# A two-layer expert MLP on one core: the last product of three layer-0 pairs is made due at 16.5 instead of 18 units

## The chip, the cores and the metric

The kernel runs on one core of one Trainium2 chip. The metric is the time of one execution on the device in microseconds (us), lower is better; the time given for a kernel is the median of several executions. The engines are named as in the profile: PE (TensorE, matmuls), PEld (its weight loads), DVE (VectorE), ACT (ScalarE), POOL (GpSimd), SP (SyncE, which issues most DMAs). PSUM is the accumulator memory that PE writes, in banks; SBUF is the working memory of all the engines.

## The reference, cut to what matters

```python
# x: (16, 256, 256); cond: (16, 8); hidden sizes 512 (layer 0) and 1024 (layer 1)
# layer 0: one expert for each batch, chosen by argmax
expert = argmax(cond, -1)
up   = einsum('bsd,bhd->bsh', x, W_up[expert])   + b_up[expert]
gate = einsum('bsd,bhd->bsh', x, W_gate[expert]) + b_gate[expert]
x = x + einsum('bsh,bdh->bsd', silu(up) * gate, W_down[expert]) + b_down[expert]
# layer 1: the two best experts of eight for each batch, weighted, and a shared MLP
mlp = lambda x, g, u, d: (gelu(x @ g) * (x @ u)) @ d
x = x + sum_k w[b, k] * mlp(x, skill[sel[b, k]]) + mlp(x, shared)
```

All of it is float32.

## The kernel before, in words

**Pairs.** Batches that use the same expert are put together two at a time (`Pair`); leftovers run alone (`Single`). The order of the batches is sorted on the chip. For a pair each weight product is a 2x2 block product, and the kernel makes it with seven products and some sums instead of eight products (Strassen's way, in Winograd's form; the table `STEPS`, lines 40 to 48, gives for each of the seven steps its PSUM bank tag, its weight block and its data block). Two kinds of such products follow each other:

- the first product (gate and up together), in quarters `j` of the hidden size: 2 quarters in layer 0, 4 in layer 1. `Pair.up(j, k)` (line 533) is step k of quarter j. In this text it is **Uk**. It takes two matmuls by the program, four by the profile's count, and afterwards issues copies on ACT (`copy`, line 522) or combinations on DVE (`combine`, line 526: `c<-cp,Y` or `c<-cp,Q`).
- the last product, `Pair.down(k)` (line 587), here **Dk**, k = 0 to 6. Its matmuls are on line 597. D0, D2 and D4 all add into the one bank with tag A, D1 and D5 open a bank with tag Y (two in turn, shared with U1 and U5), D3 and D6 use the one bank B. After D0, D2 and D4 the helper `early` reads the bank A into a `dz` tile, in layer 0 on DVE (line 614, which adds the bias and x). After D1, D4, D5 and D6 the helper `late` adds the other bank and writes `ys` (line 630 in layer 0, DVE). So D2 cannot start before the `early` of D0 has read bank A, and a U1 or U5 that gets D1's bank cannot start before the `late` of D1 has read it.

Sums of data blocks are made by `sums_b` (lines 472 to 474, three DVE operations): for x, called by `sums_x` (line 463), and for the activations, called by `act_sums` (line 583). `act` (line 573) makes silu(up) * gate: ACT adds the biases and takes silu (line 571), in layer 1 it takes gelu (line 577), and DVE multiplies (line 580). Sums of weight blocks run on POOL (`sums_a`, lines 479 to 482; `sums_q` for the first product, `sums_d` for the last).

**The order of the work** is written out when the program is built. Each engine then works through its own queue in that order, and waits on semaphores where it needs another engine's result. `Line` (line 832) holds a clock in units: `main` runs a step, adds its time (`UP` = 2 units for one Uk) and then calls `flush`, which runs all that was put down with `later` and has come due, the earliest due first; among equals, what was put down first. The clock is a whole even number at every flush.

For a pair that starts at clock 0 (the one before it is called its predecessor), `Pair.run` (line 661) does this:

- U0 to U5 of quarter 0 end at clocks 2, 4, ... 12, of quarter 1 at 14 ... 24.
- U6 of a quarter is due 4 units after its end, `act0(1)` 3, `act` 6, `act_sums` 12.
- The sums of the next pair's x (`sums_x`) are put down at the start of quarter 1, clock 12, due 5 later, at 17 (line 878).
- D0 to D6 of the predecessor are due at `first + step * k`, with `first` 18 (line 460) and `step` 3 in layer 0 (lines 678 to 680): at 18, 21, 24, 27, 30, 33, 36. They thus run in the second half of the next pair and the first half of the one after.
- D6 also gives the tiles back (`give`, line 639), and what waits for a tile (`when_free`, line 132), for instance the load of the next weights `d` (line 418) or an `act`, is then issued.

In this row of work layer 0 has four pairs, here **P0 to P3** (`l0_pairs`, line 783), and then comes **S0**, the first pair of the shared MLP of layer 1 (`shared[0]`). In the profile P1 starts with the U0 at 41.71 us, P2 with that at 59.79, P3 with that at 78.82 and S0 with that at 97.36.

SP's queue holds, in program order, the loads of weights (`q<-wq_dram`, `d<-wd_dram`), of x, and the stores of layer 0's results (lines 453 and 454). The load of a weight tile `d` waits until the last product that read this tile is done.

Of the kernel before, what the change touches and what calls it, by code (L numbers as in the profile page):

```python
# [59 lines left out]
def kernel(  # L60
# [722 lines left out]
    l0_pairs = [Pair(next(names), 0, 2 * i) for i in range(NP1)]  # L783
# [4 lines left out]
    pairs = [Pair(next(names), 1, 2 * i) for i in range(NP2)]  # L788
    more_pairs = [Pair(next(names), 1, 2 * NP2 + 2 * i) for i in range(MOST[1])]
    ones = [Single(next(names), 1, 2 * NP2 + i) for i in range(NS2)]  # L790
    shared[-1].last = True
    shared[-2].step = 7

# [307 lines left out]
```

## Time and profile before

| what | value |
|---|---|
| median of 3 runs | 1051.12 us (1050.55 to 1052.24) |
| the profiled execution, its time | 1051.36 us |
| the profiled execution, its span | 1049.7 us |
| PE busy | 1038.2 us, 99% of the span |
| PEld busy | 900.3 us, 86% |
| DVE busy | 777.0 us, 74% |
| ACT busy | 371.3 us, 35% |
| POOL busy | 446.7 us, 43% |
| granted PE clock | 0.999 |

The span runs from the first to the last instruction; the time of the same execution is 1.66 us longer. A busy time is the sum of an engine's instructions. Matmuls are pipelined and their ends are modelled, so it is better to look at their starts: from one step of four matmuls to the next there are 0.864 us where nothing is waited for (89.59, 90.45, 91.31 for U1, U6, U2 of P3), and any larger distance is a wait. A line of the timeline gives the start, the duration, the engine, the line of the program, the operation with output <- inputs, the shape, the count of merged instructions and, in brackets, the idle time ahead of it with what ended it.

### The profile page before, as it was taken

Reading aid. Unit: us, or ns where it says so; the run is one execution under the profiler, and the core shown is the slowest. Engines: PE = TensorE matmul, PEld = TensorE weight load, DVE = VectorE, ACT = ScalarE, POOL = GpSimd, SP = SyncE. Lnnn points to the kernel's source line nnn. Section 1 sums busy time; section 2 is a strip of 40 time slices with the busy share of each in tenths; the row PEclk is TensorE's granted clock in tenths of the full one; section 3 lists DMA queues with packets and bytes.
Section 4 is the critical chain, followed back from the end, with each engine's and each line's share of the span. In section 5 each row is a group of like instructions: output and inputs, shape, how many; then the busy total and the mean of one; then the engine's idle time right before and its main releaser. Section 6 shows DMA issues by size and latency. Waiting matters only on the chain.

```text
span 1049.7 us, 14152 instructions
## 1 busy us (share of the span) xinstructions
PE 1038.2 (99%) x4750; PEld 900.3 (86%) x4750; DVE 777.0 (74%) x1207; ACT 371.3 (35%) x583; POOL 446.7 (43%) x492
## 2 busy tenths in 40 slices
PE   9999999999999999999999999999999999999998
PEld 6778888888888888888888888888888888888886
DVE  7789978878687877887777778777766236776764
ACT  2444353535333333333333333333333123333331
POOL 2946331221043765666476556645201245630000
PEclk9999999999999999999999999999999999999999
DMA  7636656656664355345335533543655445356522
GB/s 237 241 127 203 240 181 194 207 166 236 200 235 119 88 140 140 93 109 140 98 87 138 140 98 103 140 122 83 178 159 171 133 136 156 91 180 184 183 75 45
DMA packets 60974, 157.47 MB, mean 150 GB/s; under 512 B 7506, under 2 KB 27090, under 8 KB 56658
## 3 DMA queue, kind: packets, MB, share of 16 engines
q1 hardware_dynamic: 47618, 140.90, 40.3%
q0 software_dynamic: 12976, 15.21, 9.4%
q8 instruction: 42, 0.69, 0.3%
q14 instruction: 50, 0.41, 0.1%
q10 hardware_dynamic: 288, 0.26, 0.1%
HBM read 132.23 MB, written 24.12 MB: 149 GB/s over the span
## 4 chain that ended last, share of the span: by engine, by line
PE 89%; DVE 7%; issue 2%; ACT 1%; DMA 1%; SPq 0%; DVEq 0%; ACTq 0%
PE X L541 24%; PE Q L541 16%; PE Y L541 16%; PE A L597 12%; PE B L597 9%; PE Y L597 8%; DVE c L526 2%; PE X L692 2%; PE Q L692 1%; DVE bt L580 1%; PE A L722 1%; DVE bt L472 1%; DVE bt L473 1%; PE B L722 1%; ACT c L577 1%
## 5 line engine op out<-in xcount | busy, mean ns | idle before, releaser
L522 ACT ACTIVATE cp<-X 128x512 f32<-128x512 f32 x318 | 189.5, 596 | 519.2 <-PE X L541 518.6
L580 DVE TENSOR_TENSOR bt<-c 128x1024 f32<-128x1024 f32 x106 | 145.7, 1374 | 102.8 <-ACT c L577 93.0
L541 PE MATMUL Y<-xt,q 128*128 128x256 f32 x736 | 189.8, 380 | 1.1 <-DVE c L526 0.6
L541 PE MATMUL Q<-xt,s 128*128 128x256 f32 x736 | 189.5, 380 | 0.6 <-DVE c L526 0.6
L541 PE MATMUL X<-xt,s 128*128 128x256 f32 x736 | 189.5, 380 | 0.0
L526 DVE TENSOR_TENSOR c<-cp,Q 128x512 f32<-128x512 f32 x212 | 144.3, 681 | 37.4 <-ACT cp L522 32.9
L526 DVE TENSOR_TENSOR c<-cp,Y 128x512 f32<-128x512 f32 x212 | 144.1, 680 | 22.4 <-PE Y L541 22.0
L541 PEld LDWEIGHTS Y<-xt,q 128*128 128x128 f32 x736 | 138.9, 190 | 23.2 <-DVE c L526 3.9
L451 POOL DMA_DIRECT2D out_dram<-ys x46 | 49.0, 1065 | 255.7 <-DVE ys L626 103.2
L541 PEld LDWEIGHTS Q<-xt,s 128*128 128x128 f32 x736 | 139.3, 190 | 21.2 <-DVE c L526 2.5
L541 PEld LDWEIGHTS X<-xt,s 128*128 128x128 f32 x736 | 139.3, 190 | 20.5 <-ACT cp L522 1.4
L479 POOL TENSOR_TENSOR s<-q 128x256 f32<-128x256 f32 x78 | 72.1, 924 | 131.8 <-PE Q L541 66.2
L482 POOL TENSOR_TENSOR s<-s,q 128x256 f32<-128x256 f32 x78 | 62.5, 801 | 101.0 <-PE Q L541 101.0
L597 PE MATMUL A<-bt,ds 128*128 128x256 f32 x424 | 101.5, 379 | 1.4 <-DVE dz L614 1.4
L597 PE MATMUL B<-bt,ds 128*128 128x256 f32 x424 | 101.4, 379 | 0.0
L577 ACT ACTIVATE c<-c 128x1024 f32<-128x1024 f32 x92 | 96.7, 1052 | 12.9 <-DVE c L526 12.7
L472 DVE TENSOR_TENSOR bt<-bt 128x512 f32<-128x512 f32 x113 | 95.0, 840 | 0.7 <-DMA bt<-x_dram 0.6
L541 PE MATMUL X<-xt,q 128*128 128x256 f32 x368 | 94.4, 379 | 0.0
L597 PEld LDWEIGHTS A<-bt,ds 128*128 128x128 f32 x424 | 80.4, 190 | 13.0 <-POOL s L481 1.4
L597 PEld LDWEIGHTS B<-bt,ds 128*128 128x128 f32 x424 | 80.5, 190 | 11.2 <-ACT ys L737 0.3
L597 PE MATMUL Y<-bt,d 128*128 128x256 f32 x376 | 90.0, 379 | 0.0
L597 PEld LDWEIGHTS Y<-bt,d 128*128 128x128 f32 x376 | 71.4, 190 | 9.7
(163 smaller groups left out, 1157.1 us busy)
## 6 DMA issues: line engine op xcount, KB each, us to landing
q<-wq_dram SPq DMA_DIRECT2D x114, 512.0 KB, 3.7
d<-wd_dram SPq DMA_DIRECT2D x22, 1024.0 KB, 6.6
s<-qsums SPq DMA_DIRECT2D x28, 512.0 KB, 4.9
xt<-x1d SPq DMA_DIRECT2D x46, 256.0 KB, 4.3
out_dram<-ys POOLq DMA_DIRECT2D x46, 256.0 KB, 5.1
ds<-dsums SPq DMA_DIRECT2D x7, 1024.0 KB, 6.3
d<-wd_dram SPq DMA_DIRECT2D x7, 513.0 KB, 5.1
bt<-x_dram SPq DMA_DIRECT2D x14, 256.0 KB, 4.7
```

The costliest lines, as they stand in the source:

```text
L451: nc.gpsimd.dma_start(row(out), ys[:, :, t, :], accum_op=ALU.add)
L472: tt(t[:, 4:6, :], t[:, 0:3:2, :], t[:, 2:4, :], ALU.subtract)
L479: tt(s("S1"), a("A21"), a("A22"), ALU.add)
L482: tt(s("nS4"), s("S2"), a("A12"), ALU.subtract)
L522: nc.scalar.activation(t, self.banks["X", j], AF.Copy)
L526: nc.vector.tensor_tensor(self.c[j][:, block].rearrange("p m s -> p (m s)"), self.copies[n, j], self.banks[tag, j], op,)
L541: nc.tensor.matmul(self.banks[tag, j][:, bass.ts(m, S)], lhsT=self.q[j][:, m, A_AT[a], :] if a in A_AT else self.s[j][:, m, S_AT[a], :], r ...
L577: nc.scalar.activation(u, u, AF.Gelu_apprx_tanh)
L580: nc.vector.tensor_tensor(t[:, 0:4, :], u, v, ALU.mult)
L597: nc.tensor.matmul(d, lhsT=src[:, j, :], rhs=self.acts[j][:, B_AT[b], :], start=OPENS[k] and j == 0, stop=j == self.kp - 1, skip_group_che ...
L692: nc.tensor.matmul(dst[:, bass.ts(half, S)], lhsT=self.q[j][:, m, 2 * half + c, :], rhs=self.xt[:, c, :], start=(c == 0), stop=(c == KD - 1),)
L722: nc.tensor.matmul(self.po[:, bass.ts(c, S)], lhsT=self.d[:, 2 * c + half, j, :], rhs=self.acts[j][:, bass.ts(half, S)], start=(j == 0 and ...
```

## The change

It sets the attribute `first` of the first three layer-0 pairs, P0, P1 and P2, from 18 to 16.5. P3 and all pairs of layer 1 keep 18.

```diff
     ones = [Single(next(names), 1, 2 * NP2 + i) for i in range(NS2)]
+    for u in l0_pairs[:-1]:
+        u.first = 16.5
     shared[-1].last = True
```

The due times of D0 to D6 of these pairs become 16.5, 19.5, 22.5, 25.5, 28.5, 31.5 and 34.5, counted from the start of the next pair. Since a flush happens at even clocks only, D0, D2, D4 and D6 still run in the flushes at 18, 24, 30 and 36; D1, D3 and D5 run in those at 20, 26 and 32 instead of 22, 28 and 34. Within the flush at 18, where `sums_x` is due at 17, D0 now comes ahead of it.

## Prediction

> **What bounds the kernel now.** I first read the busy times of the page and then the busy time by stretches.
>
> ```profile
> PE 1038.2 (99%) x4750; PEld 900.3 (86%) x4750; DVE 777.0 (74%) x1207; ACT 371.3 (35%) x583; POOL 446.7 (43%) x492
> ```
>
> PE sets the time: what counts is how long it stands still, and how long it stands still because of the steps that move. By stretches (columns: stretch, length, then busy time and instruction count of PE, PEld, DVE, ACT, POOL, granted clock, DMA share, GB/s):
>
> ```profile
> 56.60:80.00 23.40, 21.82 (x99) 17.97 (x97) 20.74 (x34) 9.64 (x17) 10.57 (x13) 1.00 0.46 146
> 80.00:97.00 17.00, 17.00 (x79) 14.98 (x80) 16.39 (x27) 8.57 (x14) 8.59 (x11) 1.00 0.62 208
> 97.00:132.00 35.00, 34.67 (x160) 29.95 (x159) 32.15 (x52) 13.95 (x20) 17.95 (x18) 1.00 0.63 226
> 132.00:1000.00 868.00, 866.66 (x3996) 757.06 (x3996) 637.32 (x943) 307.96 (x482) 371.72 (x373) 1.00 0.50 146
> ```
>
> The reader is to see two things. From 132 to 1000 us PE is idle 1.3 us of 868, so a start of layer 1 that is earlier by some time moves the end by the same time. And from 56.6 to 132 us DVE is busy 89 to 96% of the time: it is nearly a second bound there, and PE can only gain what DVE can follow. Next PE's timeline where D0 to D3 of P0 and P1 lie:
>
> ```profile
> 56.77 1.03 PE L541 MATMUL Y<-bt,q 128*128 128x256 f32 x4
> 58.85 1.10 PE L597 MATMUL A<-bt,ds 128*128 128x256 f32 x4 [1.05 <-DVE dz L614]
> 59.79 1.03 PE L541 MATMUL X<-bt,q 128*128 128x256 f32 x4
> 60.82 1.13 PE L541 MATMUL Y<-bt,q 128*128 128x256 f32 x4
> ...
> 76.46 1.03 PE L541 MATMUL Y<-bt,q 128*128 128x256 f32 x4
> 77.88 1.10 PE L597 MATMUL A<-bt,ds 128*128 128x256 f32 x4 [0.39 <-DVE dz L614]
> 78.82 1.03 PE L541 MATMUL X<-bt,q 128*128 128x256 f32 x4
> 79.98 1.13 PE L541 MATMUL Y<-bt,q 128*128 128x256 f32 x4
> ```
>
> D2 (A<-bt,ds) waits for line 614, the copy of bank A after D0, twice; the U1 after it is late again. And DVE's timeline shows why the copy is late:
>
> ```profile
> 55.62 0.95 DVE L472 TENSOR_TENSOR bt<-bt 128x512 f32<-128x512 f32 x1
> 56.61 0.83 DVE L473 TENSOR_TENSOR dz<-bt 128x256 f32<-128x256 f32 x1
> 57.47 0.83 DVE L474 TENSOR_TENSOR bt<-bt,dz 128x256 f32<-128x256 f32 x1
> 58.23 0.47 DVE L614 SCALAR_TENSOR_TENSOR dz<-A,d,bt 128x256 f32<-128x256 f32 x1
> 58.63 1.21 DVE L580 TENSOR_TENSOR bt<-c 128x1024 f32<-128x1024 f32 x1
> 59.76 0.67 DVE L526 TENSOR_TENSOR c<-cp,Q 128x512 f32<-128x512 f32 x1
> 60.36 0.41 DVE L630 TENSOR_TENSOR ys<-dz,Y 128x256 f32<-128x256 f32 x1
> ```
>
> D0 started at 53.32 and ended at 54.35, yet its copy ran at 58.23, behind the three sums of the next x. Those are wanted only by P2's U2 at 63.51.
>
> [...] line 614 starts where line 474 ends, 3.9 us after its matmuls. [...] lines 473 and 474 take 0.83 us beside POOL's sums and 0.42 when POOL is idle (62.39, 89.98), and 614, 526 and 630, each with a PSUM input, keep 0.47, 0.68 and 0.41. [...]
>
> **The change part by part.** No instruction is added or removed.
>
> *D0 ahead of sums_x.* This moves one DVE copy of 0.47 us past three sums that take 58.23 − 55.62 = 2.61 us. The copy would run at 55.62 and end at 56.09.
>
> *D1, D3, D5 one Uk earlier on PE.* PE does the same steps in another order. From D0 at 53.32 to U6 there are nine distances (D0, U3, D1, U4, U5, D2, U0, D3, U1, U6): 9 × 0.864 = 7.77, so U6 could start at 61.09. It started at 62.65: **1.56 us of stalls**. For P1's D0 at 73.01 the same nine end at 80.78 instead of 81.82: **1.04 us**. D0 to D6 of P2, beside P3, have no stall to lose (from 79.98 to 115.49 all distances are 0.864).
>
> *Do the stalls go?* First window: D2 could start at 57.63, with its copy done at 56.09. The sums then run from 56.02; POOL stops at 58.03, so line 474 is partly free of it (saved: between 0 and 0.4), and line 580 ends its slot between 59.4 and 59.8. Line 630 of D1 now comes ahead of `c<-cp,Q` (D1 is flushed before U4) and is done at 59.8 to 60.2. The U1 that wants its bank comes at 60.23, one step later than it would have, because D3 is put ahead of it. Stall left: 0 to 0.1, I take 0. Second window, PE now 1.56 earlier: DVE idles 0.97 and 1.21 us at 64.5 and 67.2 waiting for PE and ACT, so it follows, by about 1.4 at line 580 (70.09 becomes 68.7). There the copy runs at 73.5, D2 at 75.76; line 630 is done at 78.0, U1 comes at 78.35. Stall left: 0 to 0.2, I take 0.
>
> *What is late next.* From about 69 us DVE has almost no idle time, so it stays 1.4 to 1.5 us ahead of its old times while PE is 2.60 ahead. In P3's window I compared each PE wait with the DVE operation it hangs on: D6 at 85.26 against line 630 done at 84.52; U1 at 86.99 against 86.4; U6 at 87.85 against 87.0; D6 of the next at 103.39 against 102.66. All hold, by 0.6 to 0.9 us. At S0's first `act` it does not quite hold. Gelu waits for the table load (from PE's U2, so 2.60 earlier: ends 112.46 − 2.60 = 109.86) and for DVE's `c<-cp,Q` (ends 111.57, less 1.45: 110.12, plus some 0.05 until ACT sees it). The second is later by 0.3. From gelu the chain goes over line 580 (113.56), `c<-cp,Q` (115.78) and line 630 (116.38) to the U1 at 116.84, which already waits; P3's own steps are not moved, so that stall of 0.59 stays and grows by these **0.3 us** (0 if POOL leaves DVE freer, 0.9 if DVE falls back to 0.85 ahead).
>
> *Other queues.* The order on ACT, POOL and SP is the same. D5 is the last reader of a `d` tile, so SP's load of the next one (68.12 and 87.29) comes some 2.4 and 3.5 us earlier, and POOL's sums of it (71.86, 91.35, which start when it lands) with it. Nothing waits for them. But they meet other DVE operations: in the P3 window they leave sums_x and fall on `act_sums` (89.98, 90.44), each 0.41 us slower or faster per operation, in sum zero; bounded by 0.8 either way. The `dz` tiles change hands in another order; five are there and at most four are held. The sums of x are 0.47 later: U2 wants them at 61.96, they are done by 58.7.
>
> *Sum.* 1.56 + 1.04 − 0.3 = 2.3, with about 0.05 for the bounded ends, which lean to the gain through line 474: **2.35 us**. Against the profiled execution, 1051.36 (span 1049.7 and 1.66 around it), that is 1049.0; it lies 0.24 above the median, so for the median 1051.12 − 2.35 = **1048.8**. Between 2.0 and 2.7 us are this case's own ends.
>
> **The rivals.**
>
> *DVE gives back the second stall.* It is 96% busy from 80 to 97. If POOL's sums cost it 0.8 us more and it gets to S0 only 0.65 ahead, gelu is late by 1.1 and the gain is 1.5: **1049.6**. For it: the slacks of 0.6 to 0.9 above. Against it: the POOL work is as much as before.
>
> *It doesn't do what it says.* The profile also names POOL beside D2's weight load ("PEld A L597 <- POOL s L481: 1.4", ending 58.03). If that were the wait, D2 would start at about 58.1 and the gain in the first window be some 0.95, in the second 0.65: **1049.5**. Against it: D2's weight sums were made at 47.64 on POOL, ten us before; and POOL's operation had ended 0.8 us before PE went on, while line 614 ended 0.15 before.
>
> *Slower.* POOL's sums, moved by 2.4 to 3.5 us, fall on DVE operations between 66 and 111 us that are free of them now. Their price is read from the trace: line 580 goes from 1.22 to at most 2.29 (113.56), lines 473 and 474 from 0.42 to 0.83. There are three such line 580 (70.09, 86.21, 104.44) and two such pairs (89.98, 108.36): 3 × 1.07 + 4 × 0.41 = 4.9 us. DVE would be at S0 3.4 us later than before instead of 1.45 earlier, and since gelu has 0.85 of slack over it today, the kernel 2.6 us slower: **1053.7**. It decides from a loss of 2.3 us on; below that the change still gains. Against it: POOL would have to hit every one, and leave the ones it hits now.
>
> *More than forecast.* The stall of 0.59 at S0 goes too, because POOL's long sum (114.74, 2.25 us) lies otherwise against line 580: **1048.2**.
>
> **How the numbers follow.** Forecast 0.72, DVE gives back 0.12, not the wait that is named 0.05, slower 0.05, more 0.06. About 0.2%, 2.1 us or 1049.0, is what a measurement of this kernel can tell from no change. The forecast's own ends of 2.0 to 2.7 straddle it; I put three quarters of it beyond: 0.54, and with the last case 0.60 faster. The other quarter, 0.18, and the first two rivals make 0.35 the same, and 0.05 slower. The range goes from 1047.9 (the case of more, with 0.3 for the spread of a median) to 1050.3 (DVE giving back all but 0.8 us); the slower case is left out.
>
> **What would show it.** Right: line 614 ahead of 472 in three windows; D2 0.864 after U5 at about 57.6 and 75.8; U1 without a wait near 60.2 and 78.3; S0's U0 near 94.8 instead of 97.36; the wait at S0's U1 of 0.6 to 0.9; from there the same tail, earlier by 2.3. Wrong: a D2 that still waits, for POOL; or new waits of PE for `c<-cp,Q` or line 630 between 84 and 105, or gelu at S0 waiting for DVE by over 1 us.

## The result, and the profile after

| | before | changed |
|---|---|---|
| median | 1050.68 us (14 runs, 1049.51 to 1052.29) | 1048.61 us (14 runs, 1046.97 to 1049.98) |
| profiled execution: span | 1049.7 us | 1047.3 us |
| ratio of times | | 0.9979, 95% interval 0.9972 to 0.9987 |

The change made the kernel about 2.1 us faster, 1.4 to 2.9 by the interval. The sum of the prediction was 2.35. (The 14 runs before contain the 3 of the table at the top.) PE runs the same instructions and is busy 0.9 us less; the other 1.5 us of the span were idle time. Since ends of matmuls are modelled, a part of a wait is booked as busy (the wait at 58.85 before is 1.05 us in the bracket and 1.22 by the starts), so the starts decide:

```profile
PE 1037.3 (99%) x4750; PEld 900.6 (86%) x4750; DVE 776.8 (74%) x1207; ACT 371.1 (35%) x583; POOL 449.1 (43%) x492
```

PE's timeline of the changed kernel at the two windows (start, duration, line, output <- inputs; at the granted clock of 1.00 that both windows had, a distance over 0.864 between starts is a wait):

```profile
56.73 1.03 PE L541 MATMUL Y<-bt,q 128*128 128x256 f32 x4
57.59 1.03 PE L597 MATMUL A<-bt,ds 128*128 128x256 f32 x4
58.46 1.03 PE L541 MATMUL X<-bt,q 128*128 128x256 f32 x4
59.32 1.03 PE L597 MATMUL B<-bt,ds 128*128 128x256 f32 x4
60.18 1.03 PE L541 MATMUL Y<-bt,q 128*128 128x256 f32 x4
...
75.72 1.03 PE L597 MATMUL A<-bt,ds 128*128 128x256 f32 x4
76.59 1.03 PE L541 MATMUL X<-bt,q 128*128 128x256 f32 x4
77.45 1.03 PE L597 MATMUL B<-bt,ds 128*128 128x256 f32 x4
78.62 1.13 PE L541 MATMUL Y<-bt,q 128*128 128x256 f32 x4
79.59 0.59 PE L541 MATMUL Q<-bt,s 128*128 128x256 f32 x2
```

In the first window nothing waits any more. In the second D2 comes right after U5 too, but U1 is 0.31 us late (78.62 − 77.45 − 0.864). DVE shows why the first is whole and the second is not:

```profile
55.58 0.47 DVE L614 SCALAR_TENSOR_TENSOR dz<-A,d,bt 128x256 f32<-128x256 f32 x1
55.97 0.68 DVE L472 TENSOR_TENSOR bt<-bt 128x512 f32<-128x512 f32 x1
56.68 0.83 DVE L473 TENSOR_TENSOR dz<-bt 128x256 f32<-128x256 f32 x1
57.55 0.83 DVE L474 TENSOR_TENSOR bt<-bt,dz 128x256 f32<-128x256 f32 x1
58.31 1.21 DVE L580 TENSOR_TENSOR bt<-c 128x1024 f32<-128x1024 f32 x1
59.44 0.41 DVE L630 TENSOR_TENSOR ys<-dz,Y 128x256 f32<-128x256 f32 x1
...
69.90 1.11 DVE L472 TENSOR_TENSOR bt<-bt 128x512 f32<-128x512 f32 x1
...
73.86 0.47 DVE L614 SCALAR_TENSOR_TENSOR dz<-A,d,bt 128x256 f32<-128x256 f32 x1
74.25 1.11 DVE L472 TENSOR_TENSOR bt<-bt 128x512 f32<-128x512 f32 x1
...
78.16 0.41 DVE L630 TENSOR_TENSOR ys<-dz,Y 128x256 f32<-128x256 f32 x1
```

The copy (line 614) now leads the sums in both. Line 630 ends at 59.85, ahead of the U1 at 60.18; in the second window it ends at 78.57, behind the 78.31 at which U1 could have come. Two of the sums there (line 472) took 1.11 us instead of the 0.69 and 0.71 of before. Before, each of them started ahead of a sum on POOL:

```profile
71.34 0.69 DVE L472 TENSOR_TENSOR bt<-bt 128x512 f32<-128x512 f32 x1
...
74.89 0.71 DVE L472 TENSOR_TENSOR bt<-bt 128x512 f32<-128x512 f32 x1
```

```profile
71.86 0.76 POOL L479 TENSOR_TENSOR ds<-d 128x256 f32<-128x256 f32 x1 [6.25 <-DMA d<-wd_dram]
...
75.02 1.17 POOL L479 TENSOR_TENSOR s<-q 128x256 f32<-128x256 f32 x1
```

In the changed kernel POOL's sums are 1.7 to 2.6 us sooner, and POOL starts first, at 69.23 against 69.90 and at 74.09 against 74.25:

```profile
69.23 1.23 POOL L479 TENSOR_TENSOR ds<-d 128x256 f32<-128x256 f32 x1 [5.09 <-DMA d<-wd_dram]
...
74.09 0.73 POOL L480 TENSOR_TENSOR s<-s,q 128x256 f32<-128x256 f32 x1
```

Setting the steps of both traces side by side gives how much sooner each comes than before:

| step | before | changed | sooner by |
|---|---|---|---|
| P0's D0 | 53.32 | 53.28 | 0.04 |
| U6 of the first window | 62.65 | 61.05 | 1.60 |
| U6 of the second window | 81.82 | 79.59 | 2.23 |
| S0's U5 of quarter 0 | 105.13 | 102.90 | 2.23 |
| S0's U1 of quarter 1 | 116.84 | 114.12 | 2.72 |
| a U1 of layer 1 | 642.09 | 639.87 | 2.22 |
| a U1 of layer 1 | 714.66 | 712.68 | 1.98 |
| the end | 1049.7 | 1047.3 | 2.4 |

So the two windows gave 1.56 and 0.63. At S0 the kernel before had waited 0.59 us, and that went too: 0.49 of it show at the U1 of the table, the rest at the next step (117.81 before, 114.99 after: sooner by 2.82). Layer 1 then took back some 0.4. At S0, DVE's line 580 and POOL's sums of S0's weights (128x512) run at the same time, and some of these operations take about 1 us more than others of their kind (2.29 us against 1.25, 2.25 against 1.26). Before, on DVE and then on POOL:

```profile
113.56 2.29 DVE L580 TENSOR_TENSOR bt<-c 128x1024 f32<-128x1024 f32 x1 [1.59 <-ACT c L577]
```

```profile
113.51 1.26 POOL L481 TENSOR_TENSOR ds<-d 128x512 f32<-128x512 f32 x1
114.74 2.25 POOL L482 TENSOR_TENSOR ds<-ds,d 128x512 f32<-128x512 f32 x1
```

After:

```profile
111.68 1.25 DVE L580 TENSOR_TENSOR bt<-c 128x1024 f32<-128x1024 f32 x1 [0.73 <-ACT c L577]
```

```profile
110.57 1.28 POOL L480 TENSOR_TENSOR ds<-ds,d 128x512 f32<-128x512 f32 x1
111.81 2.26 POOL L481 TENSOR_TENSOR ds<-d 128x512 f32<-128x512 f32 x1
```

The reader is to compare starts and ends. Before, POOL's line 481 starts at 113.51, 0.05 us ahead of line 580, and ends at 114.77; line 580 ends 1.08 later, at 115.85, as if it had begun only then. After, line 580 starts at 111.68, 0.13 us ahead of POOL's sum, and it is POOL that ends 1.14 us after DVE's end (112.93). In both meetings the operation that started first kept its short time (1.26 us on POOL, 1.25 on DVE). Between the two traces the starts of the two operations have moved by 0.18 us against each other, and line 580 differs by 1.04 us. The same pairing exists in layer 1 (line 580 took 1.23 us at 711.13 before, 0.01 us ahead of POOL's line 480, and 1.94 at 709.49 after, 0.41 us behind it, and the U1 after it, at 712.68, was 0.19 us late). That such meetings make the table's last column fall from 2.72 to 1.98 in layer 1 is likely, but only this place was followed.

### The profile page after: what moved, and what is told of

Read it like the earlier page. It is cut to its first block, busy times and chain, and to the rows that moved or that the text cites. A ratio compares the mean times of both kernels' runs of the same rounds, so it can differ in the third digit from the quotient of the medians.

```text
span 1047.3 us, 14151 instructions
## 1 busy us (share of the span) xinstructions
PE 1037.3 (99%) x4750; PEld 900.6 (86%) x4750; DVE 776.8 (74%) x1207; ACT 371.1 (35%) x583; POOL 449.1 (43%) x492
## 4 chain that ended last, share of the span: by engine, by line
PE 87%; DVE 7%; DMA 2%; issue 2%; ACT 1%; POOL 1%; SPq 0%; ACTq 0%; POOLq 0%
PE X L541 23%; PE Q L541 16%; PE Y L541 15%; PE A L597 12%; PE B L597 9%; PE Y L597 8%; DVE c L526 3%; PE X L692 2%; PE Q L692 1%; DVE bt L472 1%; DVE bt L580 1%; DMA d<-wd_dram 1%; ACT c L577 1%; PE A L722 1%; PE B L722 1%
## 5 line engine op out<-in xcount | busy, mean ns | idle before, releaser
L526 DVE TENSOR_TENSOR c<-cp,Y 128x512 f32<-128x512 f32 x212 | 144.0, 679 | 23.2 <-PE Y L541 22.5
L482 POOL TENSOR_TENSOR s<-s,q 128x256 f32<-128x256 f32 x78 | 61.2, 785 | 99.6 <-PE Q L541 99.6
L472 DVE TENSOR_TENSOR bt<-bt 128x512 f32<-128x512 f32 x113 | 99.4, 880 | 0.9 <-DMA bt<-x_dram 0.8
L480 POOL TENSOR_TENSOR s<-s,q 128x256 f32<-128x256 f32 x78 | 78.2, 1002 | 6.1
```

Source lines behind the costliest of these rows:

```text
L472: tt(t[:, 4:6, :], t[:, 0:3:2, :], t[:, 2:4, :], ALU.subtract)
L480: tt(s("S2"), s("S1"), a("A11"), ALU.subtract)
L482: tt(s("nS4"), s("S2"), a("A12"), ALU.subtract)
L526: nc.vector.tensor_tensor(self.c[j][:, block].rearrange("p m s -> p (m s)"), self.copies[n, j], self.banks[tag, j], op,)
```

## The experiments

"Sooner by" is always against the trace of before, less the offset at P0's D0; ratios are against runs of the kernel before on the same chip. Six of them use this helper:

```diff
         first, step = 18, None
+        sooner = {}
...
-                line.later(self.first + step * k, lambda k=k: self.down(k))
+                line.later(self.first - self.sooner.get(k, 0) + step * k, lambda k=k: self.down(k))
```

**D0 alone.** Is the copy in front of the sums the whole of it?

```diff
+    for u in l0_pairs[:-1]:
+        u.sooner = {0: 1.5}
```

> Only D0 of P0 to P2 is due at 16.5; D1 to D6 stay at 21 to 36. Theory A (D2's wait for line 614 and U1's wait for line 630 are two links of one VectorE queue, and the second is opened only by D1 and D3 coming sooner): D2 starts without a wait at about 57.6, but U1 waits for line 630, which still stands behind the sums, line 580 and c<-cp,Q and ends near 60.4; U6 of the first window starts near 62.3 instead of 62.65, and the second window gains about nothing: 0.3 to 0.6 us in all. Rival B (the copy in front of the sums is the whole effect): 2.2 us at U6 of the second window, as with the change.

Measured: 1051.28 us, ratio 1.0003 (0.9995 to 1.0011): no gain, where 0.3 to 0.6 us had been expected. PE's timeline of this kernel, the two lines with a wait:

```profile
60.60 1.13 PE L542 MATMUL Y<-bt,q 128*128 128x256 f32 x4 [1.02 <-DVE ys L631]
80.45 1.13 PE L542 MATMUL Y<-bt,q 128*128 128x256 f32 x4 [1.45 <-DVE ys L631]
```

D2 no longer waits (it starts at 57.69), but U1 waits 1.02 and 1.45 us for line 630 (631 in this file). The wait has moved two steps on. From D0 to U6 the first window loses 1.29 us (1.56 before); the second loses 1.72 (1.04 before), and from 77.00 to 80.50 us, around its wait, DVE was busy all 3.50 us and POOL 3.09. Rival B falls.

**The rest alone.**

```diff
+    for u in l0_pairs[:-1]:
+        u.sooner = dict.fromkeys(range(1, 7), 1.5)
```

> D0 stays at 18, behind the sums of x; D1 to D6 of P0 to P2 are 1.5 units sooner. Theory A: D2 waits as before (start near 58.85), U1 comes a step later behind D3 and finds line 630 done; 0.2 to 0.3 us less at U6 of the first window, about 0.3 at the second: 0.4 to 0.6 us in all. A and B both leave most of the gain out; what differs is the sum of this run and the run with D0 alone: by A well under 2.2 us (the two parts need each other), by B this run gives nothing.

Measured: 1050.82 us, ratio 1.0002 (0.9995 to 1.0008). The first window is 0.28 us sooner, and the second 0.12 at its end, less than the 0.4 to 0.6 expected, since D2 waits longer there:

```profile
58.92 1.10 PE L598 MATMUL A<-bt,ds 128*128 128x256 f32 x4 [1.04 <-DVE dz L615]
78.25 1.10 PE L598 MATMUL A<-bt,ds 128*128 128x256 f32 x4 [0.96 <-DVE dz L615]
```

The median shows none of it. Each part alone is worth nothing that could be measured, both together 2.1 us. That is theory A: two waits on one queue, one behind the other.

**D0 and D1.** How much of it needs D3 and D5?

```diff
+    for u in l0_pairs[:-1]:
+        u.sooner = dict.fromkeys(range(2), 1.5)
```

> D0 and D1 of P0 to P2 1.5 units sooner, D2 to D6 as before; so D3 no longer stands in front of U1. Theory A: D2 without a wait; line 630 now ahead of c<-cp,Q, done near 59.85, but U1 already comes at 59.32: it waits some 0.55 us, so U6 of the first window is 1.0 us sooner than before, and the second window gains 0 to 0.4: 0.9 to 1.4 us in all, between the run with D0 alone (nothing) and the change (2.1). Rival B': D3 and D5 do not matter, and this gives the whole 2.1 us.

Measured: 1049.55 us, ratio 0.9992 (0.9984 to 1.0000): some 0.8 us, at most 1.7 by the interval, which just reaches no gain. U1 waits 0.42 and 0.45 us, U6 of the second window comes 1.2 us sooner:

```profile
59.96 1.13 PE L542 MATMUL Y<-bt,q 128*128 128x256 f32 x4 [0.42 <-DVE ys L631]
78.81 1.13 PE L542 MATMUL Y<-bt,q 128*128 128x256 f32 x4 [0.45 <-DVE ys L631]
```

So three links carry the gain: D0 ahead of the sums, D1 so soon that line 630 stands ahead of `c<-cp,Q`, and D3 ahead of U1, which gives the U1 that wants D1's bank one more step. D5, which moves with D3, was not tried apart; the wait that is left here is the one ahead of which D3 stands in the changed kernel. The trace lies in what A expected (0.9 to 1.4 us), the median just below; B', the whole 2.1, falls.

**P0 alone.**

```diff
+    for u in l0_pairs[:1]:
+        u.sooner = dict.fromkeys(range(7), 1.5)
```

> The change for P0 alone, so the first window alone. Theory A: U6 of the first window starts near 61.05, 1.56 us sooner. In the second window the stall stays or grows by 0.1 to 0.2, because VectorE comes 1.4 sooner and TensorE 1.56: S0 starts 1.3 to 1.5 us sooner, the median is 1.0 to 1.6 us lower unless the stall of 0.59 at S0 goes as well. Rival C (VectorE is the bound in this stretch and gives back whatever a window gains): the gain is gone by S0, the median as before.

Measured: 1049.68 us, ratio 0.9990 (0.9982 to 0.9999), 1.0 us. In the trace the first window gives 1.55, the second gives back 0.6 (D2 waits 0.96 us there, more than the 0.1 to 0.2 expected), and S0 is 0.99 us sooner, less than the 1.3 to 1.5 expected. Rival C is too strong: DVE gives back a part, not all.

**P0 and P1, not P2.**

```diff
+    for u in l0_pairs[:2]:
+        u.first = 16.5
```

> The change for P0 and P1, not for P2, whose last product lies beside P3 and had no stall in the kernel before. Theory A: what is won is won at the two windows, so S0 starts 2.0 to 2.2 us sooner, as with the change; beside P3 the old order leaves D2 and U1 only 0 to 0.4 us of slack with TensorE 2.2 us and VectorE 1.4 us sooner, so that a wait of up to 0.3 us may come back there; the median is 1.5 to 2.2 us lower than before. Rival G (P2's part is needed to hold the gain): a wait of 0.8 us or more beside P3, and a median at most 1.2 us lower.

Measured: 1047.86 us, ratio 0.9974 (0.9965 to 0.9984); S0 starts 2.18 us sooner, with no wait of PE beside P3, so rival G falls. P2's part of the change shows no effect on the time, as predicted; the gain comes with P0's and P1's.

**D1 still sooner.** The 0.31 us left in the second window should go if line 630 stood ahead of line 580 as well.

```diff
+    for u in l0_pairs[:-1]:
+        u.sooner = {**dict.fromkeys(range(7), 1.5), 1: 3.5}
```

> The change, and D1 of P0 to P2 due at 17.5, so that it is issued in the flush at 18 right after the sums of x and its copy (line 630) stands in front of line 580. Theory A: in the second window the U1 that waited 0.31 us for line 630 in the changed kernel no longer waits, U6 there starts 2.6 us sooner than in the kernel before instead of 2.2; at S0 gelu then waits some 0.75 us for c<-cp,Q instead of 0.35, so that up to 0.4 us is given back there if that chain ends last: 2.2 to 3.0 us against the kernel before. Rival C: S0 starts no sooner than with the change.

Measured: 1052.28 us, ratio 1.0018 (1.0011 to 1.0024): slower than before, where 2.2 to 3.0 us of gain had been expected. DVE's and PE's timelines of this kernel:

```profile
77.43 2.21 DVE L581 TENSOR_TENSOR bt<-c 128x1024 f32<-128x1024 f32 x1
...
109.54 2.29 DVE L936 TENSOR_TENSOR z<-ats 128x1024 f32<-128x1024 f32 x1
...
114.14 2.36 DVE L581 TENSOR_TENSOR bt<-c 128x1024 f32<-128x1024 f32 x1 [0.73 <-ACT c L578]
```

```profile
80.30 1.13 PE L542 MATMUL Q<-bt,s 128*128 128x256 f32 x4 [0.88 <-DVE c L527]
...
117.48 1.13 PE L542 MATMUL Y<-xt,q 128*128 128x256 f32 x4 [1.95 <-DVE ys L631]
118.45 1.44 PE L598 MATMUL B<-bt,ds 128*128 128x256 f32 x4
119.68 1.91 PE L542 MATMUL Q<-xt,s 128*128 128x256 f32 x4
```

U1 is free in the second window, but U6, next in line, waits 0.88 us for `c<-cp,Q`: line 580 (581 here), now behind line 630, started at 77.43 instead of 77.02, ran beside POOL and took 2.21 instead of 1.21. At S0 DVE met POOL twice more (2.29 and 2.36 instead of about 1.2), gelu waited 1.99 us for DVE, and U1 1.95. After that PE itself was slow, at a granted clock of 0.58 from 118.45 to 121.40. By stretches (length; busy time of PE, PEld, DVE, ACT, POOL; granted clock; DMA):

```profile
114.00:117.48 3.48, 1.53 (x9) 0.99 (x7) 3.34 (x4) 1.19 (x3) 1.98 (x3) 1.00 1.01 311
118.45:121.40 2.95, 2.95 (x10) 2.36 (x9) 2.88 (x5) 0.00 (x0) 0.00 (x0) 0.58 0.50 203
```

The clock was 0.50 from 119 to 121 us and 0.67 from 121 to 123, and the four steps from 117.48 to 122.72 took 5.24 us, 1.68 more than the same four before (116.84 to 120.40). Against before, this kernel was 1.45 us sooner when S0 began and 2.3 us later at 122.72.

The timed runs show the same in part of the cases. In 9 of the 19 the mean clock of the run was 0.997 or 0.998 (an estimate from the stretches at 119 to 123 us: what this profile lost there lowers the mean by 0.0016), with a median of 1053.35 us. In the other 10 it was 0.999 or 1.000, as in every run of all the other kernels here, with a median of 1051.88. So the clock seems to cost some 1.5 us in about half of the runs, and without it this kernel is still some 1.1 us slower than before.

**Is it POOL at S0?** S0's weights for the last product loaded half a pair later, so that POOL sums them from 119 us on instead of from about 109 us. First with the kernel just shown:

```diff
-            if j == 0 and u is not l0_first:
+            if j == (2 if u is shared[0] else 0) and u is not l0_first:
```

> The kernel with the change and D1 at 17.5, which was 0.18% slower than the kernel before, with the same later load at S0. Theory D (it lost its time at S0: a route step of 2.29 and a line 580 of 2.36 us, each held up by POOL, a stall of 1.95 us and then a TensorE clock of half speed for some 3 us): both take 1.2 to 1.3 us, the stall is gone or below 0.3, the clock stays full, and the median is 1.6 to 2.4 us below the kernel before, 3 us or more below the same kernel with the early load. Rival F (D1 so soon harms in the windows themselves): it stays slower than before, or gains under 1 us.

Measured: 1049.20 us, ratio 0.9986 (0.9979 to 0.9993). The same kernel with the early load had 1.0018, so POOL's sums at S0, with what followed from them, the clock too, cost 0.32%, 3.4 us. DVE's timeline:

```profile
108.91 1.21 DVE L936 TENSOR_TENSOR z<-ats 128x1024 f32<-128x1024 f32 x1
112.44 1.23 DVE L581 TENSOR_TENSOR bt<-c 128x1024 f32<-128x1024 f32 x1 [0.73 <-ACT c L578]
```

Both operations are short, PE loses no more than 0.2 us at S0, and its granted clock is 1.00 from 112 to 124 us. The gain of 1.5 us lies a little below the expected 1.6 to 2.4, since U6's 0.88 us in the second window remains (8.81 us from D0 to U6, as before, so that this window gives nothing): D1 so soon also harms by itself (rival F, in part). The same edit with the changed kernel:

> The changed kernel with the same later load at S0. Theory D: in the changed kernel's profile that stall had gone already, because there line 580 started first; so nothing is left to gain at S0 in that profile (0.1 us or less in the place of S0's steps), and the median lies 0 to 0.4 us below the changed kernel's, if in some runs POOL comes first there; about 2.1 to 2.6 us below the kernel before.

Measured: 1047.99 us, ratio 0.9974 (0.9966 to 0.9982). The changed kernel's own ratio, 0.9979, lies inside the interval: it is not shown that this one is better. And with the kernel before:

> The kernel before, but S0's last-product weights are loaded half a pair later, so that POOL's four long sums of them run after 120 us instead of from 111 to 117. Theory D (at S0 the U1 waits because line 580 takes 2.29 us, held up by a POOL sum of weights that started first; who comes first is chance): line 580 takes 1.2 to 1.3 us, U1 comes 0.864 after U0 without a wait, all after it 0.59 us sooner, the median 0.3 to 0.9 us lower. Rival E (the wait comes from the table load and gelu, which are late anyway): line 580 shorter or not, the stall stays at 0.4 us or more.

Measured: 1050.73 us, ratio 1.0001 (0.9993 to 1.0010). The trace does what D says: line 580 takes 1.23 us, the wait is gone, S0's steps after it come 0.59 us sooner.

```profile
113.59 1.23 DVE L580 TENSOR_TENSOR bt<-c 128x1024 f32<-128x1024 f32 x1 [1.11 <-ACT c L577]
```

The median shows nothing of it, but its interval goes from 0.7 us of gain to 1.0 of loss, so that 0.59 us could be hidden in it. It is open whether the timed runs of the kernel before have that wait at all (of two other profiles with S0 within 0.5 us of its old time, that with D0 alone had none and that with the rest alone had it), whether it is paid later, or whether the noise covers it. E falls by the trace; D holds for the profile and is not shown for the median.

**P3 as well, with the later load.**

```diff
+    for u in l0_pairs:
+        u.first = 16.5
```

> The changed kernel with P3 as well at 16.5 and with S0's last-product weights loaded half a pair later. There are no sums of x to pass beside S0; D1, D3 and D5 of P3 come one step sooner. Theory D: with POOL out of the way nothing waits at S0 already, so this is the same as the changed kernel with the later load alone, 2.3 to 2.9 us below the kernel before, within 0.5 us of it. Against it: if gelu, some 0.35 us behind, still set something at S0, this one would be 0.3 to 0.5 us lower at the steps after S0's U1.

Measured: 1048.32 us, ratio 0.9982 (0.9975 to 0.9988), below the expected 2.3 to 2.9 us and not separable from the changed kernel. No gain by P3 is seen. No version was shown to beat the change.

## Why the prediction was right, step by step

- *D0 ahead of sums_x:* right. Line 614 ran at 55.58 (55.62 predicted) and D2 came without a wait. But D0 alone is worth nothing; the prediction's sum already counted D1 and D3 at U1, and that was needed.
- *First window, 1.56 us:* measured 1.56.
- *Second window, 1.04 us, "Stall left: 0 to 0.2, I take 0":* this step failed in size. 0.41 us were left (0.31 at U1, 0.10 in getting going again), so it gave 0.63. Line 614 was to run at 73.5 and ran at 73.86, line 630 was to be done at 78.0 and was done at 78.57. POOL's sums of `d` came 2.6 us sooner (69.23 instead of 71.86; 2.4 predicted) and started ahead of the line 472 at 69.90; those of `q` behind them started ahead of that at 74.25. The two took 0.8 us more. The prediction had bounded that effect by 0.8 us for P3's window and left it out for P2's.
- *Beside P3, "All hold":* right. From 80 to 117 us PE has no wait.
- *S0, 0.3 us given back:* the wait of gelu was right, 0.35 us (110.59, ahead of it `c<-cp,Q` until 110.55). That it would end last was wrong: line 580 took 1.25 instead of 2.29 us, and the wait of 0.59 went instead of growing to 0.9. That was the rival "more than forecast", by the mechanism it names.
- *Layer 1, the same time carried to the end:* nearly. It took back 0.4 us in this trace; that its meetings of line 580 with POOL did it was followed at one place only.
- *Sum:* 1.56 + 0.63 + 0.59 − 0.4 = 2.4 in the profile, the prediction 2.35. The second window and layer 1 came out 0.4 lower each and S0 0.9 higher, so that the agreement of the sum is in part luck. The timed runs, 2.07 (1.4 to 2.9), don't tell the terms apart, and that the 0.59 at S0 is in them is not shown: taking that wait away by itself did not move the median.
- *The rivals:* "DVE gives back" is seen in P0 alone, for 0.6 us. "The wait that is named" is refuted: D2 starts at 57.59, 0.5 us ahead of the end of POOL's line 481. "Slower" did not come with this change, but its mechanism is what made D1 at 17.5 slower: three DVE operations lengthened by about 1 us each, and gelu's slack used up. It does not name the clock of PE, to which 1.7 of the 3.7 us went that this kernel lost at S0 in its profile.

## What to carry to other kernels

When a wait is caused by an operation that stands behind others in its engine's queue (here the copy, which started 3.9 us after its matmuls ended), look for the next consumer of the same queue before moving it: here the first wait, taken away alone, came back two steps later (1.29 of 1.56 us in the first window, more than before in the second); two links moved together gave some 0.8 us, three gave 2.1. Where DVE and POOL met at S0, their starts moved by 0.18 us against each other between the two traces, and the operation of DVE went from 2.29 to 1.25 us; price such places from both sides in every stretch that shifts. The rank of a schedule among its neighbours can hang on them, as with D1 at 17.5, which, by the ratios, was 3.4 us faster with one load at another time.

## What was not expected of the hardware

With D1 at 17.5 a wait of 1.95 us for PE, in a stretch in which it was busy 1.53 of 3.48 us, was followed by a granted clock of 0.50 to 0.67 between 119 and 123 us, and the four steps from its end on took 1.68 us more than before. With D0 alone PE had waited 1.45 us, busy 2.05 of 3.50 us, and its clock stayed at 1.00. By their mean clock, 0.997 or 0.998 in 9 of 19, about half of the timed runs with D1 at 17.5 had the fall too. What decides it is not shown.

In the kernel with D1 at 17.5 line 580 started at 77.43, before POOL's sum at 77.81, and still ended only at 79.64, 1.09 us after that sum's end at 78.55; so who started first does not tell here who took longer. POOL had been issuing a DMA from 77.20 to 77.79. In the changed kernel POOL issued it from 77.13 to 77.72, and line 580, which started ahead of it, at 77.02, took 1.21 us. Whether the DMA has a part in this was not tried.
